# A grouped 1-D convolution of a scan kernel: eight 64-row products of some pairs replaced by a ScalarE write under the 128-row products and a VectorE add

## The chip, the cores and the metric

The kernel runs on one core of a Trainium2 chip. The metric is the device time of one execution in microseconds (us), lower is better. In the profile, PE is TensorE (the matrix engine), PEld its weight loads, DVE VectorE, ACT ScalarE, POOL GpSimd and SP SyncE, which issues nearly all DMAs from one queue. Each engine takes its instructions in the order in which they are written.

## The reference

Input x is (4, 128, 96, 96). It is group-normalised and read as four sequences per image: by rows, by columns, and both reversed. Each sequence goes through the same block, and the four results are joined by a 1x1 convolution and added to x:

```python
t = _grouped1x1(x, in_proj_w, in_proj_b, G)            # G = 4, 512 channels out
u, gate = (t[:, :HID], t[:, HID:])                     # HID = 256
u = jax.nn.silu(u)
u = lax.conv_general_dilated(u, dw_w, padding=[(2, 2)], feature_group_count=HID, ...)  # 5 taps, each channel alone
s = _conv1x1(u, ssm_in_w)                              # 32 channels
a = DMIN + (DMAX - DMIN) * jax.nn.sigmoid(_conv1x1(u, ssm_delta_w, ssm_delta_b))
bb, cc = tanh(_conv1x1(u, ssm_b_w, ssm_b_b)), tanh(_conv1x1(u, ssm_c_w, ssm_c_b))
prefix = jnp.cumsum(jnp.log(a), axis=-1)
hst = jnp.exp(prefix) * jnp.cumsum(bb * s * jnp.exp(-prefix), axis=-1)
u = u + _conv1x1(cc * hst + ssm_d[None, :, None] * s, ssm_out_w)
u = _grouped1x1(u * jax.nn.sigmoid(gate), mix_w, mix_b, G)
return _conv1x1(u, out_proj_w, out_proj_b)
```

The change concerns the 5-tap convolution alone.

## The kernel before

**Units and pairs.** The work is cut into eight phases (four images, each by columns, then by rows). A phase handles a sequence and its reverse together, in six steps of 16 lines. Within a step the positions are sorted by their remainder p modulo 4, in the order p = 1, 2, 3, 0 (`TURN`), so a step has four pairs of units (the forward and the reversed sequence). There are 192 pairs; "pair t" is number t of all, and t modulo 24 its place in a phase. A step's first pair has p = 1, the second p = 2. The reversed sequence meets the data of the first three steps again in the last three, so the in-projection and its silu (`fresh`) are computed in three steps of a phase only.

**The convolution.** Half of the 256 channels have their taps on DVE (`taps`, L730, four adds and a first tap on ACT). The other half is done on PE. Silu's output `sil` holds, on 128 partitions, the four remainders of 32 channels at a time, so one product of 128 rows with a banded matrix (`band`) gives the taps that fall into one block of four positions (`conv`, L651, eight products of 32 columns). The taps that fall into the neighbouring block are one row block for p = 0 and 3, and two for p = 1 and 2. For p = 0 and 3 ("alone") the one tap is added by DVE (`add_lone`, L684, one 128x768 multiply and add that also writes u), from the tile `lone`, in which the outer rows of `sil` stand as DMA brings them through DRAM. For p = 1 and 2 PE adds the two taps by eight products of 64 rows (`conv_less`, L700, matrix `less`), and ACT copies the finished sum to u (`copy_u`, L711).

**The order of a pair** is written out by hand in `pair_on` (L955): instructions of several pairs stand interleaved. In the pairs that the change touches (in-projection four pairs ahead not needed: places 8 to 19) the sums of `conv` use banks 6 and 7, and so do two of the four gate products of the pair before (L557), which ACT's tanh of 128x768 (L599) reads. PE does, in this order: the 128-row products; the products with `w_fin` of an older pair (L854), first half; the 64-row products; second half; gate products L557 mixed with products L577 of another pair; and the projection of u (L777, 32 records with `main`), which opens the next stretch. ACT does the first tap of the next pair (L742), the tanh L599, and then the three reads of the projection (L781, L784, L790). DVE does four taps (L744), the edge tap (L691) where there is one, half a scan in the first two pairs of a step (L819), statistics for the next image in some phases (L445) and the two gatings (L638).

**SP.** At the head of a step's first pair SP issues the load of `lone` (L682, 770 KB). In the step before the last of a phase, two loads of `sil` from DRAM (L513, 770 KB each) stand ahead of it.

## Time and profile before

| what | value |
|---|---|
| median of 3 runs | 1737.48 us (1737.05 to 1737.89) |
| span of the profiled execution (first to last instruction) | 1735.2 us |
| time around the span, median less span | 2.3 us |
| PE busy | 1713.6 us, 99% |
| DVE, ACT, POOL busy | 1507.9, 1494.8, 1447.0 us |
| DMA moved | 363.66 MB, 62.8% of the 16 DMA engines on SP's queue |

The profiled execution has no timed value of its own beside its span; the timed runs stand 2.3 us above it. Times in rows of the trace are us from the span's start. A row of the timeline gives start, duration, engine, line, operation, what is written and read, and how many instructions were merged; a bracket at its end is the idle time of the engine before it and what ended it. PE's products have two records each. In the groups by line the numbers behind the bar are busy time, mean ns of one, and idle time before.

### The profile page before, as it was taken

The page shows a single profiled execution, that of the slowest core. Times are in us where ns is not written, and L with a number is a line of the kernel's source. Part 1 is how long each engine was busy: PE and PEld are TensorE (multiplying, and loading weights), DVE is VectorE, ACT ScalarE, POOL GpSimd, SP SyncE. Part 2 cuts the span into 40 slices and gives each one's busy share as a digit, 9 for nine tenths or more (in the row PEclk, how much of TensorE's full clock was granted, in tenths as well). Part 3 has the DMA queues.
Part 4 walks back from the last instruction along what each step waited for, and adds up shares of the span by engine and source line. Part 5 has one row for each costly group of instructions (what it writes and reads, how often), then busy time and mean ns, then how long its engine had stood idle before and what let it go on. Part 6 is the DMA issues. An engine that isn't in the chain of part 4 may idle for free.

```text
span 1735.2 us, 54226 instructions
## 1 busy us (share of the span) xinstructions
PE 1713.6 (99%) x22522; PEld 644.7 (37%) x22522; DVE 1507.9 (87%) x1508; ACT 1494.8 (86%) x2544; POOL 1447.0 (83%) x1490
## 2 busy tenths in 40 slices
PE   7999999999999999999999999999999999999998
PEld 4333333343333433344333443334333333333333
DVE  6899998888889998888889999888888888888887
ACT  4888988889888888888988888888998889888875
POOL 3689889888789988888788988887878889887887
PEclk9999999999999999999999999999999999999999
DMA  7746865358884786337896487433887548643364
GB/s 244 235 147 218 288 202 151 124 206 280 275 287 139 262 267 194 118 126 263 260 308 226 150 300 251 144 123 132 294 294 239 179 144 304 201 137 133 147 226 166
DMA packets 154644, 363.66 MB, mean 210 GB/s; under 512 B 19104, under 2 KB 120864, under 8 KB 154400
## 3 DMA queue, kind: packets, MB, share of 16 engines
q1 hardware_dynamic: 154256, 360.16, 62.8%
q8 instruction: 178, 2.92, 0.7%
q14 instruction: 66, 0.54, 0.1%
q10 hardware_dynamic: 144, 0.04, 0.0%
HBM read 221.41 MB, written 138.53 MB: 207 GB/s over the span
## 4 chain that ended last, share of the span: by engine, by line
PE 95%; DVE 2%; ACT 1%; DMA 1%; issue 0%; SPq 0%; DVEq 0%; ACTq 0%
PE psum L130 81%; PE psum L577 8%; PE psum L557 5%; DVE psum L744 1%; PE psum L1188 0%; DMA acc<-in_xr 0%; DMA kept<-shared 0%; DVE u L638 0%; ACT psum L589 0%; ACT psum L742 0%; DVE u L744 0%; ACT sil L527 0%; SPq L335 0%; PE psum L1195 0%; DVE u L691 0%
## 5 line engine op out<-in xcount | busy, mean ns | idle before, releaser
L744 DVE SCALAR_TENSOR_TENSOR psum<-sil,small,psum 128x768 f32<-128x768 f32 x576 | 589.1, 1023 | 42.2 <-ACT psum L742 16.8
L130 PE MATMUL psum<-u,w_fin 128*32 128x384 f32 (+1 forms) x6192 | 541.3, 484 | 1.1 <-ACT ys L860 0.4
L130 PE MATMUL psum<-u,main 128*32 128x384 f32 x6144 | 535.0, 489 | 0.5 <-DVE u L691 0.4
L638 DVE SCALAR_TENSOR_TENSOR u<-gate,psum 128x768 f32<-128x768 f32 x376 | 341.7, 950 | 150.0 <-PE psum L577 50.8
L879 POOL TENSOR_TENSOR acc<-ys,acc 128x384 f32<-128x384 f32 x375 | 411.8, 1120 | 14.0 <-ACT ys L860 1.9
L825 POOL TENSOR_TENSOR t<-t,t 64x384 f32<-64x384 f32 (+1 forms) x192 | 287.2, 1496 | 70.6 <-DVE t L819 48.3
L589 ACT COPY psum<-u 128x768 f32<-128x768 f32 x384 | 301.4, 799 | 10.5 <-DVE u L638 4.3
L130 PEld LDWEIGHTS psum<-u,w_fin 128*32 128x32 f32 x6192 | 195.2, 109 | 309.6 <-issue 235.5
L130 PEld LDWEIGHTS psum<-u,main 128*32 128x32 f32 x6144 | 180.0, 109 | 324.5 <-issue 218.3
L130 PE MATMUL psum<-sil,band 128*32 128x384 f32 x3072 | 285.3, 488 | 0.0
L792 POOL TENSOR_SCALAR t<-tm 64x384 f32<-64x384 f32 x184 | 170.8, 928 | 114.4 <-ACT tm L781 102.4
L826 POOL TENSOR_TENSOR t<-t,t 64x384 f32<-64x384 f32 (+1 forms) x192 | 233.9, 1218 | 15.1
L793 POOL TENSOR_TENSOR t<-t,tm 64x384 f32<-64x384 f32 x192 | 213.8, 1113 | 30.2 <-ACT t L784 15.5
L577 PE MATMUL psum<-t,main 32*128 32x384 f32 x1536 | 228.1, 525 | 4.2 <-ACT psum L589 4.2
L742 ACT ACTIVATE psum<-sil,small 128x768 f32<-128x768 f32 x191 | 172.6, 904 | 65.2 <-DVE u L638 61.9
L744 DVE SCALAR_TENSOR_TENSOR u<-sil,small,psum 128x768 f32<-128x768 f32 x192 | 194.9, 1015 | 6.8
L527 ACT ACTIVATE sil<-psum,bnorm 128x385 f32<-128x385 f32 x384 | 191.6, 584 | 4.0 <-DMA edge<-sil 0.9
L557 PE MATMUL psum<-x_in,wn 32*128 32x384 f32 x768 | 161.7, 498 | 0.0
L862 ACT COPY ys<-psum 128x384 f32<-128x384 f32 x288 | 132.3, 478 | 33.0 <-PE psum L130 28.3
L130 PEld LDWEIGHTS psum<-sil,band 128*32 128x32 f32 x3072 | 88.8, 108 | 171.4 <-issue 63.1
L781 ACT ACTIVATE tm<-psum,small 128x384 f32<-128x384 f32 x192 | 110.9, 578 | 14.0 <-PE psum L130 2.3
L577 PEld LDWEIGHTS psum<-t,main 32*128 32x128 f32 x1536 | 93.9, 183 | 73.7 <-issue 41.0
(108 smaller groups left out, 1512.3 us busy)
## 6 DMA issues: line engine op xcount, KB each, us to landing
gate<-kept SPq DMA_DIRECT2D x114, 768.0 KB, 5.2
kept<-gate SPq DMA_DIRECT2D x74, 768.0 KB, 3.7
sil<-sil SPq DMA_DIRECT2D x64, 770.0 KB, 6.6
lone<-edge SPq DMA_DIRECT2D x40, 770.0 KB, 7.5
x_in<-in_xs SPq DMA_DIRECT2D x250, 96.2 KB, 3.3
edge<-sil SPq DMA_DIRECT2D x96, 192.5 KB, 3.6
out<-acc SPq DMA_DIRECT2D x46, 384.0 KB, 6.4
acc<-in_xr SPq DMA_DIRECT2D x39, 384.0 KB, 6.4
```

The lines of the kernel that those rows point to most:

```text
L130: nc.tensor.matmul(o[r, : rhs.shape[-1]], lhsT, rhs, start=start, stop=stop, skip_group_check=True)
L527: nc.scalar.activation(sils[step][:, s, j, g, :], bank(bk)[:, : N + 1], AF.Silu, bias=bn[:, 1:2] if j else bn[:, 4 + g : 5 + g],)
L557: nc.tensor.matmul(bank(to)[:, :N], stats[un["b"]][0][r, s, :], x_in[s][r, q, off : off + N], start=True, stop=True)
L577: nc.tensor.matmul(bank(ssm(bi, s) + j)[:, :N], w_so[r, bass.ts(j, P)], z[r, :], start=(bi, s) not in seeded, stop=True, skip_group_check= ...
L589: nc.scalar.copy(psum[:, ssm(bi, s) : ssm(bi, s) + 2, :N], us[bi][:, s])
L638: nc.vector.scalar_tensor_tensor(v, g, 1.0, pz, ALU.add, ALU.mult)
L742: nc.scalar.activation(part, src, AF.Copy, scale=w_tap[:, 0:1])
L744: nc.vector.scalar_tensor_tensor(us[i][:, :, 1, :] if k == K - 1 else part, src, w_tap[:, k : k + 1], part, ALU.mult, ALU.add,)
L793: nc.gpsimd.tensor_mul(ta[0:64, p, :], tb[0:64, :], tm[0:64, :])
L825: engine.tensor_mul(ta[0:64, p, r], tb[64:P, r], ta[64:P, p, r])
L826: engine.tensor_add(tb[0:64, r], ta[0:64, p, r], tb[0:64, r])
L879: adder.tensor_add(part, y, part)
```

## The change

In the second pair (p = 2) of each step at places 8 to 19 of a phase (places 9, 13 and 17, 24 pairs in all) the 64-row products and ACT's copy of u are gone. At the end of the pair before, ACT writes one tap, scaled, into banks 6 and 7 (`seed`). The 128-row products accumulate onto it (`onto`), and DVE adds the other tap from `lone` (`add_lone`), which writes u. The rows for ACT's tap come from the middle of `sil`: eight DMAs per step copy them to a new tile `middle`, four at the head of the third pair of the step before, two at that of the fourth, and two at the head of the step's first pair.

To make room for `middle`, the `xs` tiles for the statistics go from three to two, `less` from four matrices to two, and two small set-up matrices move into the tile `shared`, which is made earlier.

```diff
-            if (b, c) not in loaded and len(chunks) < 3:
+            if (b, c) not in loaded and len(chunks) < 2:
...
+    def paired(t):
+
+        return 8 <= t % NP < 20 and units[2 * t]["p"] == 2
+
+    def seed(i):
+        step = units[i]["step"]
+        nc.scalar.activation(
+            psum[:, 6:8, :N], columns(step, middle[step], 0), AF.Copy, scale=w_edge[:, 1:2]
+        )
+
-    def conv(i, banks, alone=False):
+    def conv(i, banks, alone=False, onto=False):
...
-                   True, alone)
+                   not onto, alone)
...
+    def copy_middle(step, g):
+        if step % NS not in (2, 3, 4):
+            return
+        if g == 0:
+            middle[step] = wk.tile([P, 2, N + 1], F32, tag="middle", bufs=1, name=f"middle_{step}")
+        for s, q in enumerate((2, R - 1 - 2)):
+            nc.sync.dma_start(
+                middle[step][32 * g : 32 * g + 32, s, :],
+                sils[step][32 * q : 32 * q + 32, s if fresh(step) else 1 - s, 0, g, :],
+            )
...
-            w_edge[:, 1 - k : 2 - k],
+            w_edge[:, 2:3] if p == 2 else w_edge[:, 1 - k : 2 - k],
...
+    def middles(t):
+
+        step, k = divmod(t, R)
+        if k == 0:
+            copy_middle(step, R - 1)
+        elif k == 2:
+            copy_middle(step + 1, 0)
+            copy_middle(step + 1, 1)
+        elif k == 3:
+            copy_middle(step + 1, 2)
...
-        single = alone(un["p"])
+        both = paired(t)
+        single = alone(un["p"]) or both
...
+        middles(t)
...
-        conv(i, banks, single)
+        conv(i, banks, single, both)
...
+        if paired(t + 1):
+            seed(i + 2)
```

Three places of the program show what moved, all at pairs 16 and 17 of the first phase (step 4; `u_0_4_1` is u of pair 16, `u_0_4_2` of pair 17).

PE, from the projection of pair 16 to the first products of the next group, before:

```order
L130 MATMUL psum_72<-u_0_4_1_0_1793,main_130 32x384 x16
L130 MATMUL psum_72<-sil_1_447,band_142 32x384 x8
L130 MATMUL psum_72<-u_0_2_3_0_1249,w_fin_144 32x384 x8
L130 MATMUL psum_72<-sil_1_447,less_143 32x384 x8
L130 MATMUL psum_72<-u_0_2_3_0_1249,w_fin_144 32x384 x8
L557 MATMUL psum_72<-x_in1_71,wn_0_269 128x384
```

and in the changed kernel:

```order
L130 MATMUL psum_72<-u_0_4_1_0_1801,main_130 32x384 x16
L130 MATMUL psum_72<-sil_1_442,band_142 32x384 x8
L130 MATMUL psum_72<-u_0_2_3_0_1249,w_fin_144 32x384 x16
L562 MATMUL psum_72<-x_in1_71,wn_0_264 128x384
L582 MATMUL psum_72<-t1_0_2_0_0_1400,main_130 128x384 x3
```

The eight 64-row products (`less`) between the two halves of `w_fin` are gone; nothing else moved on PE.

ACT, from the gate reads of pair 16 to the evacuations of pair 17, before:

```order
L742 ACTIVATE psum_72<-sil_1_447,small_91 128x2x384
L599 ACTIVATE gate1_177<-psum_72,bnorm_0_272 128x2x384
L781 ACTIVATE tm_0_4_1_0_1880<-psum_72,small_91 128x384
L784 COPY t1_0_4_1_0_1863<-psum_72 64x384
L790 ACTIVATE t1_0_4_1_0_1863<-psum_72,small_91 64x384
L802 ACTIVATE t1_0_3_0_0_1761<-t1_0_3_0_0_1761,small_91 64x384
L589 COPY psum_72<-u_0_2_0_0_1335 128x2x384
L862 COPY ys_0_2_3_0_1915<-psum_72 128x384
L589 COPY psum_72<-u_0_2_0_0_1335 128x2x384
L717 COPY u_0_4_2_0_1890<-psum_72 128x2x384
L862 COPY ys_0_2_3_1_1936<-psum_72 128x384
```

and in the changed kernel:

```order
L765 ACTIVATE psum_72<-sil_1_442,small_92 128x2x384
L604 ACTIVATE gate1_172<-psum_72,bnorm_0_267 128x2x384
L662 ACTIVATE psum_72<-middle_4_1609,small_92 128x2x384
L804 ACTIVATE tm_0_4_1_0_1887<-psum_72,small_92 128x384
L807 COPY t1_0_4_1_0_1870<-psum_72 64x384
L813 ACTIVATE t1_0_4_1_0_1870<-psum_72,small_92 64x384
L825 ACTIVATE t1_0_3_0_0_1767<-t1_0_3_0_0_1767,small_92 64x384
L594 COPY psum_72<-u_0_2_0_0_1339 128x2x384
L885 COPY ys_0_2_3_0_1923<-psum_72 128x384
L594 COPY psum_72<-u_0_2_0_0_1339 128x2x384
L885 COPY ys_0_2_3_1_1935<-psum_72 128x384
```

The copy to `u_0_4_2` is gone, and the write from `middle_4` stands ahead of the three reads of the projection, behind the tanh that reads the same banks.

SP at the head of pair 16, from the store of the last gate to the next, before:

```order
L1066 DMA kept0_10_188<-gate0_176 128x1536
L513 DMA sil_5_1787<-sil0_0_202 128x1540
L513 DMA sil_5_1787<-sil0_1_203 128x1540
L682 DMA lone_4_1790<-edge0_1_211 128x4x385
L437 DMA xs_1_15_1810<-in_xr 128x384
L323 DMA x_in0_70<-in_xs 64x385
L323 DMA x_in1_71<-in_xs 64x385
L1066 DMA kept0_11_189<-gate1_177 128x1536
```

and in the changed kernel:

```order
L1104 DMA kept0_10_183<-gate0_171 128x1536
L518 DMA sil_5_1793<-sil0_0_197 128x1540
L518 DMA sil_5_1793<-sil0_1_198 128x1540
L705 DMA lone_4_1796<-edge0_1_206 128x4x385
L687 DMA middle_4_1609<-sil_1_442 32x385 x2
L329 DMA x_in0_70<-in_xs 64x385
L329 DMA x_in1_71<-in_xs 64x385
L1104 DMA kept0_11_184<-gate1_172 128x1536
```

The last two of the eight copies to `middle_4` stand right behind the loads of `sil` and `lone`; the `xs` load, of which there are now fewer ahead, has left this place.

More of the change, by code (lines that the diff above doesn't have):

```diff
@@ L131, in mm, with shared @@
                          skip_group_check=True)
-    gmeans = wp.tile([P, 2, P], F32, name="gmean")
-    gmean = gmeans[:, 0, :]
+    rp = ctx.enter_context(tc.tile_pool(name="shared", bufs=1))
+    def shared():
+        return rp.tile([P, 16 * P], F32, tag="shared", name="shared")
+    w_out_fuse = shared()
+    gmean = wp.tile([P, P], F32, name="gmean")
+    gmeans = (gmean, w_out_fuse[:, 15 * P : 16 * P])
     per = DIM // GN_GROUPS
@@ L148, in conv_preact_kernel @@
     for e in range(2):
-        nc.gpsimd.tensor_copy(gmeans[:, 1, bass.ts(e, 64)], gmeans[:, 0, bass.ts(1 - e, 64)])
+        nc.gpsimd.tensor_copy(gmeans[1][:, bass.ts(e, 64)], gmean[:, bass.ts(1 - e, 64)])
     gmask = wp.tile([P, 4], F32, name="gmask")
@@ L192, in stats_first @@
         for e in range(2):
-            product(pv[:, e : e + 1], gmeans[:, e, :], ex)
+            product(pv[:, e : e + 1], gmeans[e], ex)
         var = sp.tile([P, 2], F32, tag="var", name=f"var_{b}")
@@ L337, in load_x @@
                 nc.vector.bn_stats(stats_of(b0)[:, e, :], accf[:, bass.ts(e, SC)])
-    rp = ctx.enter_context(tc.tile_pool(name="shared", bufs=1))
-    def shared():
-        return rp.tile([P, 16 * P], F32, tag="shared", name="shared")
     b0 = phases[0][0]
@@ L351, in conv_preact_kernel @@
     load_x([(0, 1), (1, 1), (2, 1), (3, 2), (5, 2), (7, 3), (10, 4), (14, 4), (18, 4), (22, 2)])
-    w_out_fuse = shared()
     nc.sync.dma_start(w_out_fuse[:, 0 : 2 * HID + 4 * P], fuse)
@@ L362, in conv_preact_kernel @@
     d_sb, b_mix, b_out, b_fuse = (w_small[:, a:b] for a, b in ((79, 80), (80, 82), (82, 83), (83, 84)))
-    w_edge = w_small[:, 84:86]
+    w_edge = w_small[:, 84:87]
     w_out = w_out_fuse[:, 0:HID]
@@ L374, in less_of, with alone @@
         return 1 if p < 2 else 0
+    def alone(p):
+        return p in (0, R - 1)
     def less_rows(s, p):
@@ L380, in conv_preact_kernel @@
     band = wp.tile([P, 2, R, 4, 32], F32, name="band")
-    less = wp.tile([P, R, 4, 32], F32, name="less")
+    less = wp.tile([P, 2, 4, 32], F32, name="less")
     w_fin = wp.tile([P, 4, 2, P], F32, name="w_fin")
     b_fin = wp.tile([P, 1], F32, name="b_fin")
-    id32 = wp.tile([P, 32], F32, name="id32")
+    id32 = w_out_fuse[:, 13 * P : 13 * P + 32]
     ident = w_out_fuse[:, 2 * HID + 4 * P : 2 * HID + 5 * P]
@@ L394, in conv_preact_kernel @@
                 if k == less_of(p):
-                    r, to = less_rows(s, p), less[:, p]
+                    if alone(p):
+                        continue
+                    r, to = less_rows(s, p), less[:, p - 1]
                 m = R * k - p + R - 1
@@ L433, in load_chunks @@
         for b, c in ahead:
-            if (b, c) not in loaded and len(chunks) < 3:
+            if (b, c) not in loaded and len(chunks) < 2:
                 loaded.add((b, c))
-                chunks[b, c] = wk.tile([P, SC], F32, tag="xs", bufs=3, name=f"xs_{b}_{c}")
+                chunks[b, c] = wk.tile([P, SC], F32, tag="xs", bufs=2, name=f"xs_{b}_{c}")
                 nc.sync.dma_start(chunks[b, c], xr[b, :, bass.ts(c, SC)])
@@ L657, in conv @@
                 mm(bank(b0 + s), g, band[:, s, p, g, :], columns(step, sil[s][:, g, :], 1 - k),
-                   True, alone)
-    def alone(p):
-        return p in (0, R - 1)
+                   not onto, alone)
     edge_sil = [
@@ L666, in conv_preact_kernel @@
     ]
-    lone = {}
+    lone, middle = {}, {}
+    def copy_middle(step, g):
[8 more added lines that the diff above has]
+            )
     def edge_of(step):
@@ L705, in conv_less @@
                 r = less_rows(s, p)
-                mm(bank(b0 + s), g, less[r, p, g, :], columns(step, sil[s][r, g, :], k),
+                mm(bank(b0 + s), g, less[r, p - 1, g, :], columns(step, sil[s][r, g, :], k),
                    False, True)
@@ L724, in less_both @@
                 r = less_rows(s, p)
-                mm(bank(banks[s]), g, less[r, p, g, :], columns(step, sil[s][r, g, :], k), False, True)
+                mm(bank(banks[s]), g, less[r, p - 1, g, :], columns(step, sil[s][r, g, :], k), False, True)
     def new_u(i):
@@ L1050, in pair_on @@
             if gated % NP > 2:
-                both = to[:, :, 0]
+                low = to[:, :, 0]
             else:
                 spot = 2 - shift
-                both = to[:, spot : spot + 2]
-            tanh_into(gated, both, 0, psum[:, 6:8, :N])
+                low = to[:, spot : spot + 2]
+            tanh_into(gated, low, 0, psum[:, 6:8, :N])
+        if paired(t + 1):
+            seed(i + 2)
         if un["order"] == "V" and un["b"] + 1 < B and un["st"] == NS - 1 and k == R - 1:
@@ L1067, in pair_on @@
             else:
-                nc.sync.dma_start(keep(gated)[:, :, 0], both)
+                nc.sync.dma_start(keep(gated)[:, :, 0], low)
         load_kept(n + 2)
@@ L1338 @@
         v["fuse_b"],
-        v["dw_w"].reshape(HID, K)[:P, [K - 1, 0]],
+        v["dw_w"].reshape(HID, K)[:P, [K - 1, 0, 1]],
     ]
```

## The prediction

> **What bounds the kernel now.** I read the first part of the page, then the chain that ended last, then the stretch around the changed pairs engine by engine.

> ```profile
> PE 1713.6 (99%) x22522; PEld 644.7 (37%) x22522; DVE 1507.9 (87%) x1508; ACT 1494.8 (86%) x2544; POOL 1447.0 (83%) x1490
> PE 95%; DVE 2%; ACT 1%; DMA 1%; issue 0%; SPq 0%; DVEq 0%; ACTq 0%
> ```

> TensorE (PE) is busy in 99% of the span and carries 95% of the chain that ended last. So a product that goes away is worth its whole place on PE, and any new wait of PE costs its whole length. The groups by line give the price of what goes and comes (the 64-row products, VectorE's add of an edge tap):

> ```profile
> L130 PE MATMUL psum<-sil,less 64*32 64x384 f32 x1536 | 84.1, 495 | 0.0
> L691 DVE SCALAR_TENSOR_TENSOR u<-lone,small,psum 128x768 f32<-128x768 f32 x96 | 96.8, 1009 | 2.5 <-PE psum L130 1.4 <-ACT gate L593 1.1
> ```

> The kernel already has pairs without 64-row products: the third and fourth of a step. PE's order of time from a second pair (61, its projection at 561.44) to the third (62, its projection at 569.70) shows both kinds:

> ```profile
> 552.33 2.79 PE L130 MATMUL psum<-u,main 128*32 128x384 f32 x32
> 554.93 1.47 PE L130 MATMUL psum<-sil,band 128*32 128x384 f32 x16
> 557.62 0.88 PE L130 MATMUL psum<-sil,less 64*32 64x384 f32 x16
> 561.44 2.79 PE L130 MATMUL psum<-u,main 128*32 128x384 f32 x32
> 564.04 1.47 PE L130 MATMUL psum<-sil,band 128*32 128x384 f32 x16
> 569.70 2.79 PE L130 MATMUL psum<-u,main 128*32 128x384 f32 x32
> ```

> Pair 61 takes 561.44 - 552.33 = 9.11 us, pair 62 takes 569.70 - 561.44 = 8.26 us, and neither has a gap on PE. The 128-row products ("band") start 2.60 us after a projection starts, which is when the projection has streamed.

> **Removed: 64-row products.** The change takes them out of 24 pairs (three in each of eight phases). Each such pair loses 9.11 - 8.26 = 0.85 us on PE: 24 x 0.85 = **-20.4 us**, if nothing else makes PE wait. The group's own busy time says the same, 84.1 us over 96 pairs, or 0.88 each. [...]

> **Moved on ScalarE (ACT): the new write ("seed").** The copy L717 leaves the middle of the pair, and a scaled write of 128x768 into banks 6 and 7 comes to the end of the pair before, behind the tanh L599 that reads those banks and ahead of the three reads of the projection. L742 is the same kind of write. ACT at pair 60's end, and the same read of the projection by ACT for pair 61, at 563.62, with ACT's next idle time:

> ```profile
> 553.11 0.91 ACT L742 ACTIVATE psum<-sil,small 128x768 f32<-128x768 f32 x1
> 553.95 0.88 ACT L599 ACTIVATE gate<-psum,bnorm 128x768 f32<-128x768 f32 x1
> 554.73 0.57 ACT L781 ACTIVATE tm<-psum,small 128x384 f32<-128x384 f32 x1
> 563.62 0.58 ACT L781 ACTIVATE tm<-psum,small 128x384 f32<-128x384 f32 x1
> ...
> 566.87 0.48 ACT L862 COPY ys<-psum 128x384 f32<-128x384 f32 x1 [0.17 <-PE psum L130]
> ```

> The band products of pair 61 write banks 6 and 7, so today they may start once L599 is over: 553.95 + 0.88 = 554.83, and they start at 554.93. With the seed they accumulate onto it. It can start where L781 starts now, 554.73, takes 0.90 and ends at 555.63; PE follows an ACT result within 0.07 us (1434.70 + 0.88 to 1435.65, rows below), so band starts at 555.70 instead of 554.93: PE waits **0.77 us**. In the phases of the other order ACT is a little earlier:

> ```profile
> 342.54 0.89 ACT L599 ACTIVATE gate<-psum,bnorm 128x768 f32<-128x768 f32 x1
> 343.75 1.47 PE L130 MATMUL psum<-sil,band 128*32 128x384 f32 x16
> ```

> The seed would run from 342.54 + 0.78 = 343.32 to 344.22, and band would start at 344.30 instead of 343.75: **0.55 us**. Thirteen of the 24 places have nothing worse than this: all eight at pair 13 of a phase, and five at pair 9. Five of them read like the first stretch and eight like the second: 5 x 0.77 + 8 x 0.55 = **+8.3 us**. ACT's later reads (L781 and on) then start 0.14 us before band, against 0.42 at 563.62 (band at 564.04); 0.17 of the lag of 0.28 falls into ACT's idle time before L862 and 0.11 reaches PE through the copy that the products L577 wait for: 24 x 0.11 = **+2.6 us**.

> **Added on VectorE (DVE): one L691 in each of the 24 pairs, 1.01 us.** It stands between the last tap and the scan:

> ```profile
> 557.22 1.01 DVE L744 SCALAR_TENSOR_TENSOR u<-sil,small,psum 128x768 f32<-128x768 f32 x1
> 558.26 1.81 DVE L819 TENSOR_TENSOR_SCAN t<-t 64x768 f32<-64x768 f32 x1
> 560.96 1.82 DVE L638 SCALAR_TENSOR_TENSOR u<-gate,psum 128x768 f32<-128x768 f32 x2 [0.88 <-PE psum L577]
> ```

> The gating L638 now idles 0.88 us for PE. With L691 the scan ends at 560.07 + 1.01 = 561.08, and PE, 0.77 later and 0.85 shorter, delivers at about 560.99. DVE is 0.1 us late, which the 0.25 us between ACT's tanh and the next band absorb: no cost. Behind L691 stand the scan and, for GpSimd (POOL), the outputs that read it; their result is needed a pair later. If the cover is gone, DVE would add up to 1.0 us per pair.

> **Added on SP's queue: the rows that the seed reads.** They are staged by eight copies of 48 KB per step, SBUF to SBUF. The seed waits for all of them, and the last two are issued at the head of the very pair at whose end the seed runs. In pairs 64, 40, 160 and the like (pair 16 of a phase) they stand on SP right behind two loads of `sil` and the load of `lone`, 770 KB each. Pair 40/41, SP first, then the times from issue to landing (the third of these rows is the median over the run), then the seed's neighbours:

> ```profile
> 371.00 0.44 SPq L682 DMA_DIRECT2D lone<-edge  x1
> 371.54 1.30 SPq L323 DMA_DIRECT2D x_in<-in_xs  x2
> ...
> lone<-edge SPq DMA_DIRECT2D x1, 770.0 KB, 8.4
> x_in<-in_xs SPq DMA_DIRECT2D x2, 96.2 KB, 8.1
> x_in<-in_xs SPq DMA_DIRECT2D x250, 96.2 KB, 3.3
> ...
> 377.29 0.89 ACT L599 ACTIVATE gate<-psum,bnorm 128x768 f32<-128x768 f32 x1
> 378.49 1.47 PE L130 MATMUL psum<-sil,band 128*32 128x384 f32 x16
> ```

> `lone` lands at 379.4. The small `x_in` loads behind it, 96 KB each, land at about 379.8 and 380.2: they need 8.1 us where such a load takes 3.3 in the median, so they queue behind the big ones. The copies will stand between: landing at about 379.65. The seed, ready at 378.1, then starts at 379.7, and band at 379.7 + 0.90 + 0.07 = 380.7 instead of 378.49: 2.2 us. Pair 160/161 is the longest of those whose landing the trace has:

> ```profile
> 1428.17 0.45 SPq L682 DMA_DIRECT2D lone<-edge  x1
> ...
> lone<-edge SPq DMA_DIRECT2D x1, 770.0 KB, 10.3
> x_in<-in_xs SPq DMA_DIRECT2D x2, 96.2 KB, 10.0
> ...
> 1434.70 0.88 ACT L599 ACTIVATE gate<-psum,bnorm 128x768 f32<-128x768 f32 x1
> 1435.65 1.48 PE L130 MATMUL psum<-sil,band 128*32 128x384 f32 x16
> ...
> 1434.00:1436.00 2.00, 2.00 (x31) 0.69 (x27) 1.86 (x3) 2.00 (x4) 1.86 (x3) 1.00 1.05 391
> ```

> The last row is that of 2 us: the DMA engines are full (share 1.05, 391 GB/s). `lone` lands at 1438.5, the copies with it, band at 1438.5 + 0.1 + 0.97 = 1439.6 instead of 1435.65: 4.0 us. I take 2.8, nearer the shorter, since 10.3 us is the longest landing of `lone`: 8 x 2.8 = **+22.4 us** (ends: 16 at 2.0 each, 32 at 4.0). In the three phases that reload the accumulator, pair 8 has the same pile. There one load behind `lone` bounds it:

> ```profile
> 513.79 0.52 SPq L437 DMA_DIRECT2D xs<-in_xr  x1
> xs<-in_xr SPq DMA_DIRECT2D x1, 192.0 KB, 7.7
> 518.99 0.89 ACT L599 ACTIVATE gate<-psum,bnorm 128x768 f32<-128x768 f32 x1
> 520.18 1.48 PE L130 MATMUL psum<-sil,band 128*32 128x384 f32 x16
> ```

> The copies land before 513.79 + 7.7 = 521.5, so band starts at the latest at 522.6, a wait of 2.4 us; at the least it is the 0.55 of ACT alone. I take the middle: 3 x 1.5 = **+4.5 us** (1.7 to 7.2).

> **Edits of no cost.** Two `xs` buffers for three: a load is issued after the last read and has a pair, 8.3 us, to land. The smaller set-up on POOL and the shared tile are done in the first 12 us, when PE waits for data. `lone` is read a pair earlier: in pair 160/161 it lands at 1438.5 and would be read at about 1441, after the late band.

> **Sum**, against the span of 1735.2 us of the profiled execution: -20.4 + 8.3 + 2.6 + 4.5 + 22.4 = +17.4, or 1752.6. The median of the timed runs is 2.3 us longer than that span; the same 2.3 around the new span gives **1755 us**. With the ends of the two DMA terms and the small lag at nothing the sum runs from -20.4 + 8.3 + 1.7 + 16 = +5.6 to -20.4 + 8.3 + 2.6 + 7.2 + 32 = +29.7: 1743 to 1767.

> **Rivals.** (1) *The copies do not queue; a small copy between SBUF addresses lands as `edge` does:*

> ```profile
> edge<-sil SPq DMA_DIRECT2D x96, 192.5 KB, 3.6
> ```

> Then all 24 places cost ACT's wait alone, 24 x 0.64 = 15.4, and the sum is -20.4 + 15.4 + 2.6 = -2.4, or 1735; without the lag 1732.5. The point at which it decides is a landing by 378.1 in pair 41, 6.5 us after the issue. Against it stand the 8.1 and 10.0 us of the loads in the same places. Chance 0.09, about half of it faster by more than 0.2% (3.5 us, about what a measurement tells from no change) and half within it. (2) *PE runs slower after the new waits.* PE's first products, after 11.66 us without work, and some 8 us later:

> ```profile
> 11.66 5.49 PE L1188 MATMUL psum<-acc 128*128 128x512 f32 x6 [11.66 <-DMA acc<-in_xr]
> 19.69 0.68 PE L1188 MATMUL psum<-acc 128*128 128x256 f32 x2
> ```

> That is 5.49 / 6 / 512 = 1.79 ns per column, then 0.68 / 2 / 256 = 1.33: a slow stretch of 5.5 us loses 1.4 us. If each of the eight long waits brings one, 8 x 1.4 = 11 us more, 1766. No wait inside the run of before is long enough to show it. [...] Chance 0.10. (3) *DVE becomes the bound* in the phases with statistics: half of L691 unhidden, 24 x 0.5 = 12 us more, 1767. The 0.88 us of idle time above speaks against it. Chance 0.05.

> **Chances and range.** The forecast has 0.74, the rivals 0.09, 0.10 and 0.05, and 0.02 is left for a gain that I don't see. So faster 0.06, same 0.05, slower 0.89. The range takes in the bounds of the DMA terms and most of rivals 2 and 3: 1742 to 1768.

> **What would show it.** The group of 64-row products falls to 72 pairs' worth, some 63 us of busy time. ACT's new write idles for a DMA into `middle`, some 20 us in all, and PE's idle time before band products goes from 0.0 to over 25 us, longest at pair 17 of a phase. It would be wrong if the copies landed before ACT is ready: then the new write starts 0.78 us after L599 everywhere, and the kernel is at 1735.

## The result and the profile after

The changed kernel takes **1792.68 us** (median of 4 runs, 1792.63 to 1794.66) against 1737.43 us of the kernel before in the same measurement (1737.05 to 1737.89): the ratio is 1.032, with a 95% interval of 1.0306 to 1.0335. It is slower, as forecast, but by 55 us where 18 were forecast, and lies above the range. The span of the profiled execution went from 1735.2 to 1790.9 us.

The page of the changed kernel: busy times, then the chain that ended last.

```profile
PE 1718.4 (96%) x22138; PEld 651.2 (36%) x22138; DVE 1523.9 (85%) x1532; ACT 1498.9 (84%) x2544; POOL 1431.1 (80%) x1486
PE 82%; DMA 5%; ACT 5%; DVE 4%; issue 2%; POOL 1%; SPq 1%; ACTq 0%; DVEq 0%; POOLq 0%
```

PE has 384 instructions fewer and is busy for 4.8 us *more*. DMA, 1% of the chain before, now holds 5%, and PE 82% where it held 95%. The groups by line, with different shapes kept apart (busy time, mean ns of one, idle time ahead). The first row is the band products of the kernel before, the others are the changed kernel's:

```profile
L130 PE MATMUL psum<-sil,band 128*32 128x384 f32 x3072 | 285.3, 488 | 0.0
...
L130 PE MATMUL psum<-sil,less 64*32 64x384 f32 x1152 | 63.1, 495 | 0.0
L130 PE MATMUL psum<-sil,band 128*32 128x384 f32 x3072 | 297.1, 505 | 47.6 <-ACT psum L662 47.6
L662 ACT ACTIVATE psum<-middle,small 128x768 f32<-128x768 f32 x24 | 21.7, 905 | 34.5 <-DMA x_in<-in_xs 14.5 <-DMA middle<-sil 11.2 <-DMA kept<-gate 8.3
L714 DVE SCALAR_TENSOR_TENSOR u<-lone,small,psum 128x768 f32<-128x768 f32 x120 | 121.0, 1009 | 38.7 <-PE psum L130 38.7
```

The 64-row products fell from 84.1 to 63.1 us, as announced. PE's idle time ahead of the band products rose from 0.0 to 47.6 us, all of it waiting for ACT's new write (L662), and that write itself sat idle for 34.5 us. Three transfers are named there, but at all eleven places with a long wait the write starts 0.1 to 0.3 us behind the landing of the last copy into `middle`, so it is the copies that it waits for. And the band products became slower: 505 ns each in the mean after 488, while the `w_fin` products went from 487 to 491 and the other large groups moved by 2 ns at most.

Where the time went is seen by taking, for every pair, the time from its first band product to that of the next pair, after less before, added over the eight phases:

| place in a phase | us | each |
|---|---|---|
| 8 (ahead of the changed pair 9) | +14.17 | 0.68 or 0.87 in five phases; 3.21, 4.90, 2.47 in the three that reload the accumulator |
| 9 | -1.77 | -0.78 where nothing else happens; +0.92 and +1.95 behind two of the long waits |
| 12 | +6.38 | 0.67 or 0.92 |
| 13 | -6.20 | -0.78 |
| 16 | +31.41 | 2.76 to 4.94 |
| 17 | +7.05 | -0.78 once, else +0.53 to +1.89 |
| 22, 23 (first phase) | +3.84 | 3.44 and 0.35 |
| ahead of the first pair | +1.12 | start of the kernel |
| all others | -0.4 | |

The sum is 55.6 of the 55.7 us by which the span grew. The worst places are 16 and 17. In the first phase SP, and the times from issue to landing of those loads; then ACT and PE:

```profile
160.01 0.91 SPq L518 DMA_DIRECT2D sil<-sil  x1
160.98 0.50 SPq L705 DMA_DIRECT2D lone<-edge  x1
161.52 1.38 SPq L687 DMA_DIRECT2D middle<-sil  x2
...
lone<-edge SPq DMA_DIRECT2D x1, 770.0 KB, 10.7
middle<-sil SPq DMA_DIRECT2D x2, 48.1 KB, 10.1
```

```profile
167.50 0.88 ACT L604 ACTIVATE gate<-psum,bnorm 128x768 f32<-128x768 f32 x1
172.19 0.91 ACT L662 ACTIVATE psum<-middle,small 128x768 f32<-128x768 f32 x1 [3.81 <-DMA middle<-sil]
...
173.15 2.79 PE L130 MATMUL psum<-sil,band 128*32 128x384 f32 x16 [4.47 <-ACT psum L662]
175.71 4.33 PE L130 MATMUL psum<-u,w_fin 128*32 128x384 f32 x32
179.96 0.58 PE L562 MATMUL psum<-x_in,wn 32*128 32x384 f32 x1
```

`lone` lands at 171.6 us (10.66 after its issue), the copies behind it at 171.9 and 172.1 (10.35 and 9.79 after theirs; the row gives the middle of the two), and ACT starts at 172.19. The tanh had been done since 168.38, so 3.81 us go to the transfer. PE waits 4.47 us, and then its band products take 2.79 us where they took 1.47. The copies, issued behind the large load in the same queue, land 0.2 and 0.4 us behind it, where a copy takes 3.4 us from issue to landing in the median of the run.

Busy time in four stretches of 3.41 us there, and in two around a wait of 3.42 us in another phase (the columns behind the length: PE, PEld, DVE, ACT, POOL; then the granted clock, the DMA share and GB/s):

```profile
168.63:172.04 3.41, 0.04 (x4) 0.00 (x0) 3.06 (x3) 0.00 (x0) 2.31 (x2) 1.00 1.06 328
172.04:175.45 3.41, 2.30 (x16) 0.78 (x20) 0.00 (x0) 3.21 (x6) 1.63 (x2) 0.50 1.00 415
175.45:178.87 3.42, 3.42 (x24) 0.96 (x20) 2.78 (x2) 0.70 (x2) 0.28 (x1) 0.50 0.13 50
178.87:182.28 3.41, 3.41 (x44) 1.40 (x40) 1.25 (x3) 2.63 (x6) 3.06 (x4) 1.00 0.00 0
...
608.95:612.36 3.41, 1.95 (x26) 0.52 (x16) 3.23 (x4) 1.65 (x2) 3.27 (x4) 1.00 1.09 349
612.36:615.78 3.42, 1.47 (x20) 0.67 (x24) 1.60 (x2) 2.37 (x5) 1.65 (x2) 1.00 1.01 371
```

The granted clock is 0.50 for exactly two of these stretches, from 172.04 to 178.87, and PE's work takes nearly twice its time in them. The trace has nine such half-speed periods behind nine of the eleven long waits, 3.4 or 6.8 us long; the kernel before has one only after its last product, which ends at 1731.8 us. PE worked for some 37 us inside the nine, so about 18 us are lost: at places 9 and 17 the table shows -1.77 + 7.05 where 16 x -0.78 = -12.5 would stand, which is 17.8 us.

### The profile page after: what moved, and what is told of

It is laid out like the page before. It is cut to its first block, busy times and chain, and to the rows that moved or that the text cites. A ratio compares the mean times of both kernels' runs of the same rounds, so it can differ in the third digit from the quotient of the medians.

```text
span 1790.9 us, 53786 instructions
## 1 busy us (share of the span) xinstructions
PE 1718.4 (96%) x22138; PEld 651.2 (36%) x22138; DVE 1523.9 (85%) x1532; ACT 1498.9 (84%) x2544; POOL 1431.1 (80%) x1486
## 4 chain that ended last, share of the span: by engine, by line
PE 82%; DMA 5%; ACT 5%; DVE 4%; issue 2%; POOL 1%; SPq 1%; ACTq 0%; DVEq 0%; POOLq 0%
PE psum L130 69%; PE psum L582 7%; PE psum L562 5%; DMA middle<-sil 2%; DMA x_in<-in_xs 2%; DVE psum L767 2%; ACT psum L662 1%; DVE t L842 1%; ACT gate L604 1%; DVE u L643 1%; ACT psum L765 1%; ACT psum L594 1%; DMA acc<-in_xr 0%; DMA kept<-gate 0%; PE psum L1226 0%
## 5 line engine op out<-in xcount | busy, mean ns | idle before, releaser
L130 PE MATMUL psum<-u,w_fin 128*32 128x384 f32 (+1 forms) x6192 | 543.6, 489 | 1.1 <-ACT ys L883 0.4
L130 PE MATMUL psum<-u,main 128*32 128x384 f32 x6144 | 535.0, 489 | 0.6 <-DVE u L714 0.6
L902 POOL TENSOR_TENSOR acc<-ys,acc 128x384 f32<-128x384 f32 x375 | 417.5, 1135 | 16.3 <-DMA acc<-in_xr 3.0
L130 PE MATMUL psum<-sil,band 128*32 128x384 f32 x3072 | 297.1, 505 | 47.6 <-ACT psum L662 47.6
L130 PEld LDWEIGHTS psum<-u,w_fin 128*32 128x32 f32 x6192 | 199.5, 111 | 314.3 <-issue 254.7
L594 ACT COPY psum<-u 128x768 f32<-128x768 f32 x384 | 301.4, 799 | 10.5 <-DVE u L643 4.3
L130 PEld LDWEIGHTS psum<-u,main 128*32 128x32 f32 x6144 | 180.0, 109 | 324.1 <-issue 215.0
L582 PE MATMUL psum<-t,main 32*128 32x384 f32 x1536 | 223.6, 524 | 4.6 <-ACT psum L594 4.6
L816 POOL TENSOR_TENSOR t<-t,tm 64x384 f32<-64x384 f32 x192 | 198.6, 1035 | 30.1 <-ACT t L807 15.4
L130 PEld LDWEIGHTS psum<-sil,band 128*32 128x32 f32 x3072 | 88.4, 110 | 230.1 <-issue 67.3
L714 DVE SCALAR_TENSOR_TENSOR u<-lone,small,psum 128x768 f32<-128x768 f32 x120 | 121.0, 1009 | 38.7 <-PE psum L130 38.7
L598 ACT ACTIVATE gate<-psum,bnorm 128x384 f32<-128x384 f32 x152 | 87.9, 581 | 41.6 <-PE psum L562 30.2
## 6 DMA issues: line engine op xcount, KB each, us to landing
x_in<-in_xs SPq DMA_DIRECT2D x250, 96.2 KB, 3.0
edge<-sil SPq DMA_DIRECT2D x96, 192.5 KB, 4.1
```

Of the source, the lines that this page charges most:

```text
L130: nc.tensor.matmul(o[r, : rhs.shape[-1]], lhsT, rhs, start=start, stop=stop, skip_group_check=True)
L582: nc.tensor.matmul(bank(ssm(bi, s) + j)[:, :N], w_so[r, bass.ts(j, P)], z[r, :], start=(bi, s) not in seeded, stop=True, skip_group_check= ...
L594: nc.scalar.copy(psum[:, ssm(bi, s) : ssm(bi, s) + 2, :N], us[bi][:, s])
L816: nc.gpsimd.tensor_mul(ta[0:64, p, :], tb[0:64, :], tm[0:64, :])
L902: adder.tensor_add(part, y, part)
```

## The experiments

In the ratios, each kernel is compared with runs of the kernel before on the same chip, which stood at 1736.87 us for the first four, 1737.67 for the next three, 1737.08, 1737.41 and 1737.31 for the rest.

**Copies issued early (e_early).** The staging order changes:

```diff
-        if k == 0:
-            copy_middle(step, R - 1)
-        elif k == 2:
-            copy_middle(step + 1, 0)
-            copy_middle(step + 1, 1)
-        elif k == 3:
-            copy_middle(step + 1, 2)
+        late = (step + 1) % NS == 2
+        for g in {2: range(2 if late else R), 3: range(2, R) if late else ()}.get(k, ()):
+            copy_middle(step + 1, g)
```

> The changed kernel with the copies into middle issued earlier: for the fourth and fifth step of a phase all eight at the head of the third pair of the step before, for the third step four at the head of that pair and four at the head of the next. Nothing else differs. Theory (the eleven long waits come from copies that stand in SP's queue behind 770 KB loads, and the half clock comes from these waits): ACT's new write starts straight behind the tanh at all 24 places, 0.7 to 0.9 us of PE's idle time each; the long waits (42.0 us at places 8 and 16, of which some 9 stay) and the half clock (17.8 us) go, so 1792.7 - 33 - 17.8 = about 1742. Rival (the copies are slow wherever they stand, since the DMA engines are full): waits over 2 us stay at several places, and the time stays above 1765.

Measured: 1744.27 us, ratio 1.0045 (1.0030 to 1.0060). First the landing times of the copies in the changed kernel and in this one, then the band products, and ACT and PE at pair 60/61 of this one:

```profile
DMA to landing us min/median/max: 1.9/3.4/10.4
...
DMA to landing us min/median/max: 1.9/2.4/6.7
L130 PE MATMUL psum<-sil,band 128*32 128x384 f32 x3072 | 286.8, 490 | 16.8 <-ACT psum L662 15.2
...
560.06 0.91 ACT L765 ACTIVATE psum<-sil,small 128x768 f32<-128x768 f32 x1 [0.82 <-DVE u L643]
562.77 1.50 PE L130 MATMUL psum<-sil,band 128*32 128x384 f32 x16 [1.42 <-ACT psum L662]
```

The new write no longer waits for a DMA anywhere, and all nine half-speed periods behind it are gone (one is left, at place 22 of the first phase, below: the granted clock is 0.50 from 223.74 to 227.15 us). So some 48 of the 55 us came from the place of small copies in one queue. The 24 pairs ahead of a changed one are still 19.6 us longer in all than before, and the changed ones 16.6 us shorter. Two waits of 1.4 us stay, at place 12 of the third and the seventh phase. ACT's first tap waits for DVE's gating there, and DVE is late: its scan (L842) takes 3.8 us, where it took 3.1 in the changed kernel. What made the scan longer is not shown.

**Products in the gap (e_fill).** In the eleven pairs with a long wait PE multiplies something useless while it waits:

```diff
+FILL = 11
...
+        if i // 2 % NP == 16 or i // 2 in (2 * NP + 8, 4 * NP + 8, 6 * NP + 8):
+            for _ in range(FILL):
+                nc.tensor.matmul(bank(banks[1])[:, N:512], w_main[:, 0:P], w_main[:, 0:P],
+                                 start=True, stop=True, skip_group_check=True)
```

> The changed kernel with eleven products of 128x128 (some 0.25 us each, 2.8 us, into columns that nobody reads) on PE between the projection and the 128-row products in the eleven pairs with a long wait. The DMA waits stay as they are. Theory (half of the clock goes where PE idles more than some 2 us of a 3.4 us stretch): the granted clock stays at 1.0, PE's products behind the waits take their usual time, and 17.8 us come back less about 1 us where the wait was shorter than 2.8 us: about 1776. Rival (the slow products behind the waits come from something else, as the full DMA engines): the time stays at 1792 or a little above.

Measured: 1784.93 us, ratio 1.0273 (1.0259 to 1.0287). The same place as above, and the one half-speed period that is left behind a wait:

```profile
168.26 2.72 PE L805 MATMUL psum<-main 128*128 128x128 f32 x22
172.75 1.50 PE L131 MATMUL psum<-sil,band 128*32 128x384 f32 x16 [1.76 <-ACT psum L663]
...
1257.67:1261.08 3.41, 1.35 (x16) 0.96 (x19) 1.11 (x2) 1.42 (x3) 0.00 (x0) 1.00 1.01 416
1261.08:1264.49 3.41, 3.41 (x28) 1.14 (x23) 1.33 (x2) 2.23 (x4) 1.89 (x2) 0.50 0.55 225
```

ACT waits 3.76 us for the copies here too, and the DMA engines are as full (share 1.04 and then 0.98 from 168.63 to 175.45 us, against 1.06 and 1.00). Yet the band products take 1.50 us where they took 2.79: PE idles for 1.05 us from 168.63 to 172.04 where it idled for 3.37, and the granted clock behind it is 1.00 where it was 0.50. So the slowness was the clock, which here followed PE's own idling and not the DMA engines' load. Places 9 and 17 come back to -0.78 in ten of the eleven cases, 15.9 us in all. The time fell by 8 us and not by 16, since in the profiled execution the waits at places 8 and 16 were 4.5 us longer and that at places 22 and 23 2.3 us; why is not shown.

**Two xs buffers alone (e_xs2).** The kernel before with `len(chunks) < 2` and `bufs=2`.

> The kernel before with two xs buffers in place of three, nothing else. Theory (the third load of the pair that reads three chunks, place 22 of the first phase, waits for a buffer and VectorE for the load): one new idle stretch of PE of about 2.6 us there, 3.8 us in all: 1741.2. Rival (the buffers cost nothing, as the prediction had it, and the 3.8 us have another source): 1737.4.

Measured: 1742.10 us, ratio 1.0031 (1.0020 to 1.0042). DVE and PE at place 22 of the first phase:

```profile
216.39 1.01 DVE L445 BATCH_NORM_STATS2 bn<-xs 128x6 f32<-128x384 f32 x2
221.53 0.56 DVE L445 BATCH_NORM_STATS2 bn<-xs 128x6 f32<-128x384 f32 x1 [4.13 <-DMA xs<-in_xr]
223.87 1.32 PE L130 MATMUL psum<-x_in,wn 32*32 32x385 f32 x16 [2.51 <-DVE u L638]
```

The pair reads three chunks; the third can be loaded only when the first is read, and PE waits 2.51 us, with a half-speed period behind it (the granted clock is 0.999 in the mean of the run): 4.9 us at places 22 and 23.

**Place 13 alone (e_13).** `paired` is true at place 13 only, and copies are made for the fourth step only.

> The changed kernel with the new path at place 13 of a phase alone (8 pairs), whose copies have no pile in front of them; copies for the fourth step only. Theory (such a pair loses 0.78 us on PE and the pair before it gains 0.67 or 0.92 by waiting for ACT): 8 x 0.8 - 8 x 0.78 = +0.2 us, and the 3.8 us of the two xs buffers and up to 1 us at the start come on top: 1741 to 1743. Rival (the path costs even where its data lie ready, by added DMA traffic or VectorE's add): over 1746. Other rival (the saving of such pairs survives): under 1737.

Measured: 1742.91 us, ratio 1.0035 (1.0022 to 1.0047). Place 12 is 6.30 us longer in all, place 13 6.20 us shorter, and 7.2 us stand at places 22 and 23. Where the rows lie ready the change is worth nothing: the wait for ACT takes what PE saves.

**No pair with three chunks (e_spread).** e_early, and the plan of the first phase ends in `[LAG - 2, LAG - 1, NP - 4, NP - 3]` in place of `[LAG - 1, NP - 4, NP - 3, NP - 2]`, so the third chunk of place 22 goes to place 4.

> The kernel with the early copies, and the chunk plan of the first phase changed so that no pair reads three chunks with two xs buffers: place 22 reads two, place 4 one more. Theory (the third load alone made the stretch of 4.8 us at places 22 and 23): these places come back to the times of before and 4.8 us go, 1744.3 - 4.8 = 1739.5; what is left over the kernel before is 24 waits for ACT against 24 savings. Rival (two buffers are too few for two chunks as well): other places of the statistics phases get longer, and the time stays above 1742.

Measured: 1738.59 us, ratio 1.0009 (1.0000 to 1.0018). Places 22 and 23 are back to the times of before. What is left are 19.8 us of waits against 17.8 us of savings. (In the profiled execution, of 1742.40 us, the granted clock was 0.50 from 26.15 to 32.98 us, and the first band product came 3.9 us later than in the kernel before.)

**A tanh earlier (e_gate_mid, e_gate).** From e_spread on, the question was whether the wait for ACT can be taken away. In the pairs ahead of a changed one:

```diff
+        ahead = paired(t + 1)
+        if ahead:
+            out_of(bi, 1, 0)
+            gate_of(0, 1, 5)
         gate_of(1, 0, 7)
         gate_of(0, 0, 6)
-        out_of(bi, 1, 0)
-        gate_of(0, 1, 5)
+        if not ahead:
+            out_of(bi, 1, 0)
+            gate_of(0, 1, 5)
```

e_gate has, besides, `first_tap(i + 2)` behind `tanh_into(...)` there.

> As e_spread, and in the 24 pairs ahead of a changed one the gate product of bank 5 stands ahead of those of banks 7 and 6 on PE, so that ACT's tanh of bank 5, which waits for it, can start some 0.3 us earlier; ACT's order stays (tanh 4, tanh 5, first tap, tanh 6 and 7, new write). Theory A (the first tap is held by VectorE's gating of the banks it writes, not by the tanh before it): the new write gains nothing, 1739.5. Theory B (ACT runs without idle time from the first tanh on, so all of it moves up): 0.3 us off each of 24 waits, 1732.

> As e_gate_mid, and ACT takes the tanh of banks 6 and 7 ahead of the first tap of the next pair, so that it works while VectorE's gating still holds the banks of the tap: tanh 4, tanh 5, tanh 6 and 7, first tap, new write. Theory (the new write then ends where PE's projection ends): PE's wait ahead of the 128-row products falls from 0.7 to 0.9 us to 0.1 to 0.3 us, and 24 x 0.5 = 12 us go: about 1728, faster than the kernel before. Rival (ACT has no idle time to give there, or VectorE's taps start later by the time the first tap is moved and become the bound): 1739 or more.

Measured: e_gate_mid 1738.11 us, ratio 1.0008 (0.9999 to 1.0017); e_gate 1749.86 us, ratio 1.0082 (1.0067 to 1.0096). The first gains nothing, as theory A had it: the first tap is held by DVE. The theory of the second fell. PE and DVE at pair 13 of e_gate, and ACT at its end:

```profile
137.73 1.50 PE L130 MATMUL psum<-sil,band 128*32 128x384 f32 x16 [0.31 <-ACT psum L662]
...
136.89 3.14 DVE L767 SCALAR_TENSOR_TENSOR psum<-sil,small,psum 128x768 f32<-128x768 f32 x3 [0.60 <-ACT psum L765]
...
144.87 0.91 ACT L765 ACTIVATE psum<-sil,small 128x768 f32<-128x768 f32 x1 [0.58 <-DVE u L643]
```

The wait of PE does fall to 0.31 us. But, as its rival had it, DVE's taps start 0.60 us later, DVE's gating at the end of the pair comes later by as much, and the changed pairs get 0.58 us longer: 7.5 us gained at places 8, 12 and 16, 15.0 lost at 9, 13 and 17, 4.4 lost behind them.

**Other work for PE during the write (e_fin, e_fin_tanh).** From e_spread, in the changed pairs the first half of the `w_fin` products stands ahead of the band products, with its result in bank 2:

```diff
+        ahead = []
+        if both:
+            ahead.append(accumulate(waiting.pop(0), 2))
...
-        add_next(w[0])
+        if ahead:
+            ahead.pop()()
+        else:
+            add_next(w[0])
```

e_fin_tanh takes `first_tap(i + 2)` behind `tanh_into(...)` in the changed pairs as well.

> As e_spread, and in the 24 changed pairs the first eight w_fin products stand ahead of the 128-row products on PE and go to bank 2, which VectorE's gating has left by then, in place of bank 4; ACT's copy of their result stands ahead of its copy of u into banks 2 and 3. PE then has 1.4 us of work while ACT writes the tap. Theory (the waits for ACT's write, 0.7 to 0.9 us at 24 places, are what eats the saving): they go to 0.0, and 24 x 0.78 = 18.7 us less 2 us for the later VectorE add come out: about 1722. Rival (VectorE, with 9.1 us of work in each of the first two pairs of a step, is the next bound): the changed pair or the one behind it gets longer by 0.4 to 0.6 us, and the time is 1728 to 1735.

> As e_fin, and in the changed pairs ACT takes the tanh of banks 6 and 7 ahead of the first tap of the next pair, which waits for VectorE's gating there. Theory of e_fin: as e_fin, 1722. Rival (VectorE late): the tanh no longer stands behind the late gating, the next pair's 128-row products start on time, and this kernel is 3 to 8 us faster than e_fin.

Measured: e_fin 1739.31 us, ratio 1.0017 (1.0008 to 1.0025); e_fin_tanh 1755.24 us, ratio 1.0103 (1.0088 to 1.0119). PE in pair 13 of e_fin, and one row of ACT:

```profile
132.82 1.47 PE L130 MATMUL psum<-u,w_fin 128*32 128x384 f32 x16
134.12 1.47 PE L130 MATMUL psum<-sil,band 128*32 128x384 f32 x16
135.41 1.47 PE L130 MATMUL psum<-u,w_fin 128*32 128x384 f32 x16
138.02 0.94 PE L582 MATMUL psum<-t,main 32*128 32x384 f32 x8 [0.30 <-ACT psum L594]
...
136.34 1.53 ACT L594 COPY psum<-u 128x768 f32<-128x768 f32 x2
```

The wait for the new write is gone (the band products' idle time falls to 0.5 us in the whole run), but PE comes to the products L582 before ACT has made the copy that they add to, and the stretch of gate products and L582 takes 2.7 us in place of 1.6. The pair and the one ahead of it are together 0.07 us shorter than before in four phases and 0.03 to 0.25 us longer at most places of the others, so the theory of e_fin fell, and the next bound took even more than its rival gave it. In e_fin_tanh the next pair's band products do not start on time: DVE's taps come later, and each pair behind a changed one is 0.77 us longer. Both of its expectations fell.

**ACT relieved, then DVE relieved (e_scale, e_scale_tanh, e_less_dve).** From e_fin, ACT's `scale_s` of the pair ahead moves behind the copies of the changed pair; e_scale_tanh swaps tanh and first tap at places 9 to 19, first pairs of a step excepted; e_less_dve is e_scale with

```diff
-        taps(i, range(1, K))
+        taps(i, range(2 if both else 1, K))
```

> As e_fin, and ACT's scaling of an older pair's s (0.62 us), which stands between the reads of the projection and the copies that bank 5 and the products L582 wait for, moves behind these copies in the 24 changed pairs. Theory (with PE's wait for the new write gone, ACT is the next bound: it runs without idle time from the first tap of one pair to the last copy of the changed one, and the projection waits for it): each of these pairs loses some 0.5 us, 24 x 0.5 = 12 us, about 1727, faster than the kernel before. Rival (VectorE, 9.1 us of work in each of two pairs, sets the length of the changed pair): 1736 to 1739, and VectorE has no idle time in the first two pairs of a step.

> As e_scale, and in the second, third and fourth pairs of a step (places 9 to 19) ACT takes the tanh of banks 6 and 7 ahead of the first tap of the next pair. Theory (ACT is the bound, VectorE has slack over the four pairs of a step): the 128-row products of the next pair no longer stand behind VectorE's gating, 0 to 5 us less than e_scale. Rival (VectorE is the bound): its taps start 0.8 us later in three pairs of four, and the time rises by 15 us or more, as it did from e_fin to e_fin_tanh.

> As e_scale, but VectorE leaves out one of its four taps in the 24 changed pairs (one 128x768 multiply and add, 1.02 us; the convolution lacks one tap there). Everything else, PE's and ACT's work too, stays. Theory (with the waits for ACT gone, VectorE sets the length of the first two pairs of a step, 9.1 us each, so the saving on PE has nowhere to go): the changed pair and the one behind it get 0.4 to 0.8 us shorter together, 24 x 0.6 = 14 us, about 1724. Rival (ACT or PE is the bound and VectorE only waits): within 2 us of e_scale, 1736 to 1739.

Measured: e_scale 1737.86 us, ratio 0.9997 (0.9988 to 1.0005); e_scale_tanh 1761.67 us, ratio 1.0138 (1.0122 to 1.0155); e_less_dve 1735.74 us, ratio 0.9990 (0.9981 to 1.0000). DVE's stretch from the taps of pair 13 to those of pair 14 in e_scale (busy times as above), and ACT and PE behind it:

```profile
132.70:141.79 9.09, 9.09 (x108) 3.82 (x104) 8.81 (x8) 8.05 (x14) 7.01 (x8) 1.00 0.37 124
...
140.85 0.91 ACT L765 ACTIVATE psum<-sil,small 128x768 f32<-128x768 f32 x1 [0.51 <-DVE u L643]
142.63 1.50 PE L130 MATMUL psum<-sil,band 128*32 128x384 f32 x16 [0.24 <-ACT gate L604]
```

With the taps, the added L714, half a scan and two gatings, DVE is busy 8.81 of 9.09 us in the changed pair, with gaps of some 0.03 us between its instructions. A pair took 9.11 us before. e_less_dve takes one tap of it away (so its convolution lacks that tap), and gains some 2 us between the medians of two measurements, 1 us by the ratios, where its theory had 14; its DVE and PE at the same place:

```profile
136.78 1.01 DVE L714 SCALAR_TENSOR_TENSOR u<-lone,small,psum 128x768 f32<-128x768 f32 x1 [0.64 <-ACT ys L885]
...
135.17 1.47 PE L130 MATMUL psum<-sil,band 128*32 128x384 f32 x16
142.94 1.50 PE L130 MATMUL psum<-sil,band 128*32 128x384 f32 x16 [0.24 <-ACT gate L604]
```

DVE now idles 0.64 us ahead of the edge tap, until the band products (which stand behind the w_fin products in this version) end at 136.64; the row names ACT's copy, which the tap doesn't read. From there on, the order is the same: edge tap, scan, gating, first tap, tanh, and the next pair's band products, 0.24 us late again. So the expectation that DVE alone decides fell. The reading that is left is two bounds close together, DVE's load and the chain that starts with the late band products; that this chain is the second one follows from the order of these rows, and no run tests it by itself. No version tried beats the kernel before by more than a measurement can tell.

## Why the prediction was right and wrong, step by step

- **Saving on PE less the lag, -20.4 + 2.6.** Right: a changed pair that nothing disturbs loses 0.78 us, 24 x 0.78 = 18.7 against 17.8.
- **ACT's write at thirteen places, +8.3.** Right in mechanism, a little small: 0.67 or 0.68 us where 0.55 stood and 0.87 to 0.94 where 0.77 stood, 10.0 in all. The step "it can start where L781 starts now" was off: the new write overwrites what the tanh reads and starts 0.03 us behind the tanh's end, where L781 overlapped it by 0.10.
- **Copies in the queue at place 16, +22.4.** Right in mechanism, mis-sized: 31.4, near its upper end of 32. I took 2.8 us each, nearer the shorter landing; `lone` landed 8.5 to 10.7 us after its issue. In pair 40/41, whose 8.4 us gave the lower end, it took 10.5 us this time.
- **Copies at pair 8 of three phases, +4.5.** Mis-sized: 10.6, beyond the upper end of 7.2. That bound, a load behind `lone` that landed after 7.7 us, was the landing of one phase taken for three; in the phase of the longest wait the copies themselves needed 8.2 and 9.0 us.
- **PE slower after the waits, a rival with 0.10.** This is the step that failed: the sum of the forecast held nothing for it. It was real, at nine of eleven waits, and cost 17.8 us, 2.0 each in the mean, where the rival counted eight waits at 1.4 us, 11 in all. I had given it little, since no wait inside the run of before was long enough to show it. The first products of the kernel, at 1.79 ns per column and then 1.33, were the only row on it. They pointed the right way, but make PE slower by a factor of 1.35, where the band products behind a wait were slower by 1.9 (2.79 us against 1.47); and the profile's clock column stands at 1.00 over these first products, so that row alone does not show a half clock. Nor did the length of a wait decide it alone: one of 2.58 us brought half speed and one of 3.42 us did not, as the last section shows.
- **Two xs buffers at no cost.** Wrong: 3.8 us in this run, 4.9 in e_xs2. I looked at how long a load may take, not at the pair with three chunks, where a buffer is taken twice. The start of the kernel, 1.1 us later, was a term that the sum left out. It looks like scatter: PE's first product, which waits for a load, came 0.7 us later than before, and with the same set-up the first band product came at 30.4 us in e_13 and at 31.8 us here, against 30.7 us in the kernel before.
- **DVE's edge tap at no cost.** Not tested by this change, which hid it behind the wait for ACT. Once that wait was taken away (e_gate, e_fin, e_scale), the 0.88 us of idle time that the prediction quoted were gone: DVE's gating was late in e_gate, and in e_scale DVE was busy for 8.81 of 9.09 us. Rival 3 was a rival of the gain, more than of the forecast.

The terms as measured give -18.7 + 10.0 + 31.4 + 10.6 + 17.8 + 3.8 + 1.1 - 0.4 = 55.6 us. The range failed because it let the DMA terms or the slow clock be at their upper end, never both; but a longer DMA wait is what brought the slow clock, at nine of eleven places.

## What to carry to other kernels

Removing work from the busiest engine pays only if the engines that feed it have that much to spare in the same pair: here ACT's wait (0.7 to 0.9 us) took the whole 0.8 us, and with that wait gone, DVE and the order of the pair took it in every version tried. A small transfer that somebody waits for should be issued ahead of the large ones in its queue; moving the 48 KB copies one or two pairs forward was worth 48 us. When a change can make PE idle for 2 us or more, price the wait and the slow clock behind it together: here nine waits of 2.58 to 4.75 us were followed by half speed, at 2.0 us each in the mean.

## What the hardware showed that was not expected

```profile
1482.76:1486.17 3.41, 1.29 (x16) 0.26 (x8) 3.20 (x5) 1.50 (x3) 3.27 (x4) 1.00 1.07 351
1486.17:1489.59 3.42, 2.97 (x20) 0.99 (x24) 1.04 (x2) 3.15 (x6) 2.02 (x3) 0.50 1.03 371
```

- **Idle time is not the whole rule.** At the start of e_spread half speed came behind a window in which PE was idle for 0.16 us only, and lasted two windows, though PE had no idle time in the first. Forty of PE's 103 records in the window ahead are products of one or four columns; whether these are the reason is not shown. The window ahead and the first slow one:

```profile
22.74:26.15 3.41, 3.25 (x103) 1.79 (x111) 1.08 (x7) 2.63 (x6) 0.00 (x0) 1.00 0.53 141
26.15:29.56 3.41, 3.41 (x56) 1.48 (x38) 0.24 (x4) 3.41 (x8) 0.00 (x0) 0.50 0.22 59
```

- **The way back was stricter.** Behind the nine waits of the changed kernel, half speed lasted one window where PE idled in it for at most 0.49 us (four times) and for 0.74 us (once, at 393.91 us), and two windows where it idled for 0.98 to 2.40 us (four times).
- **The same load in the same place** took 8.4 us in one kernel and 10.5 us in the next (`lone` in pair 40), with the DMA engines full both times (shares of 0.97 to 1.13 before, 0.95 to 1.08 in the changed kernel); two us of scatter belong to a bound taken from one such landing.
